# Attention with taps of a depthwise convolution in its gaps: another account of free VectorE time, taps a step behind a chunk's first operation, the check's sums of reciprocals later

## The chip, the core and the metric

The kernel runs on one core of a Trainium2 chip. The metric is the time of one execution on the device, in microseconds (us), lower is better. The engines that matter here are TensorE (PE; its weight loads are PEld), VectorE (DVE) and ScalarE (ACT). They run side by side and wait for each other through semaphores; each takes its own instructions in the order in which the program issued them.

## What is computed

Four layers are applied one after the other to x, 16 frames of 384 channels of 16 × 16 pixels in fp32. The change concerns the first layer (attention) and the depthwise convolution of the second, which is worked on in the attention's gaps. The later layers are shortened here:

```python
# layer 0: attention over 2 groups of 8 frames, N = 8*16*16 = 2048 tokens, 12 heads of 32
qk = (xt @ qk_w.T).reshape(B, N, 2, nh, HEAD_DIM)        # q, k projected; v is x itself
attn = softmax(einsum('bhnd,bhmd->bhnm', q * scale, k))
out = einsum('bhnm,bhmd->bhnd', alpha * eye + beta * attn - gamma / N, v)
# layer 1: depthwise 7x7 convolution, layer norm over channels, MLP 384 -> 1536 -> 384
y = conv7x7_depthwise(x) + dw_b
y = layernorm(y) * ln_g + ln_b
y = gelu(y @ w1 + b1)
gx = sqrt(sum(y**2 over the frame)); y = grn_g * (y * gx / mean(gx)) + grn_b + y
x = x + y @ w2 + b2
# layer 2: Sobel filters in x and y, 768 -> 384 projection, layer norm, gelu, residual
# layer 3: 1x1, depthwise 3x3, 1x1; linear attention with 8 heads; MLP 384 -> 1536 -> 384
```

## The kernel before

The image is cut into two batches b of four blocks of 512 columns (two frames); a block has three chunks of 128 channels. The program writes out its instructions in a fixed order per engine (`InOrder`, L86), so the place where the Python code issues an instruction decides what stands behind what.

**The attention** (`attention`, L368) runs over six units u = 0 to 5. A unit is a batch and a group of four heads. Each unit has four blocks n of queries, and each block 16 steps t of 128 keys, so there are 384 steps. In a step, `scores` issues the score matmuls of four heads into two PSUM tiles `st` (three such tiles exist, of two banks each), and ScalarE takes the exponentials into two `e` tiles (eight exist, so four steps). `weighted`, issued one step later, multiplies the exponentials with the values into `av`, and VectorE adds the `e` tiles up in chunks of four steps (`ADDS`), two additions of 128 × 1024 in each step but the first of a chunk. The sums go through matmuls with ones (`weights`) into the denominators `dn`, in four parts, each issued some steps later through the table `due`, which maps a step number to functions.

At a block's end `finish` (L508) copies the denominators to `r`, and hands to `due` four inversions of 128 columns each on VectorE (indices 2 to 5 of the next block), `scale` at index 6 (va times r), and `put` at 7 (the output block). `scale` also issues the check's sum on ScalarE: an Identity over `r` into `junk` that adds up the reciprocals. These sums end in a flag that says whether a second, general version has to be run. In the steps of `SLOTS` a projection for q or k is made; it uses one of the three `st` tiles, which ScalarE (q) or VectorE (k) frees by a copy.

**The filler.** After each step `fill` (L1444) issues work of the next layer. `conv` is a task that yields operations in order: for a chunk, one operation on ScalarE (the middle tap with bias, into y) and then 48 taps on VectorE, each one `scalar_tensor_tensor` on y. In the attention it does the two first blocks, 288 taps. How many are issued at a step is set by `room`, an account in microseconds: it gains 2.25 per step and what a projection adds, loses 2.28 for the two additions and 0.8 in steps 3 to 8 of a block for the inversions, and is cut at 3.0; every operation costs 0.57. `lead` is the first block's layer 1 after its convolution (sum over channels by a matmul `su`, centring y<-su, squares, second matmul `sv`, root with two table loads, inversion of 128 × 512, product, affine); one of its operations is issued at every fourth step. `su` and `sv` take one of the `st` tiles until they are read.

**After the attention** `plan.all` (L1508) orders everything else. `Plan` (L117) keeps when each engine will be free by set costs, and the tasks are taken by start time; among those that start within `SLACK` of the earliest, the lowest `RANK` goes first. There are tasks `l1`, `mid` and `l3c` per block (layer 1, layer 2 with the first parts of layer 3, the last MLP), `conv` for the taps that are left, `prepare` for weights, and `safety` for the flag. The eight turns of the two MLPs over the blocks are fixed (`TURNS`).

Of the kernel before, what the change touches and what calls it, by code (L numbers as in the profile page):

```python
# [11 lines left out]
ALU = mybir.AluOpType  # L12
# [5 lines left out]
NC = C // P  # L18
# [10 lines left out]
NBLK = N // BLK  # L29
NIP = NBLK  # L30
NQC = N // P
SLOTS = ((0, 4, 8), (0, 4), (0, 4), (0,))
FIRST = NQC + 10
# [11 lines left out]
AFTER = ('hid', 0, 2, 1)  # L45

RANK = {
    "mid": ((-4.2, 20.2, -65.9, 40.3), (11.6, 63.7, 50.6, 36.1)),
    "l1": ((-28.5, 90.6, 6.7, 64.2), (55.1, 56.5, 16.9, 27.6)),
    "l3c": ((32.8, 24.4, 106.0, 83.3), (3.4, 80.2, 74.5, 60.5)),  # L50
    "conv": 93.3,
}
SLACK = 0.142
JUNK = 2
ADDS = ((4, 4, 4, 4), (4, 4, 4, 4))
XB, YB, SB = 12, 2, 22
TB = BLK // P
RB = 2 * HW
# [132 lines left out]
            self.step(min((s for s in starts if s[0] <= first), key=lambda s: (s[1], s[0]))[2])  # L191


class Task:


    def __init__(self, name, rank, ops):
        self.name, self.rank, self.ops = name, rank, ops
        self.head = next(ops, None)

    def advance(self):
        self.head = next(self.ops, None)


def channel_means(dve, pool, X, cols, b):
# [162 lines left out]
def attention(tc, X, xt, L0, block, small, col, cols, ones, load_qk, banks, fill, bound):  # L368
# [4 lines left out]
    pe, act, dve = (InOrder(tc, e) for e in (nc.tensor, nc.scalar, nc.vector))  # L373
    units = [(b, g) for b in range(NB) for g in range(NC)]
    with ExitStack() as actx:
# [5 lines left out]
        op = pool("op", 2)  # L381
# [44 lines left out]
        due = {}  # L426

        def unit(u, made, gm):

            b, g = units[u]  # L430
            q, keys, v = made["q"], made["k"], made["v"]
            adds = ADDS[b]
            acc, sums = {}, {}

            def scores(n, t):
                es = []
                for i in range(2):
                    es.append(ep.tile([P, 2, BLK], F32, tag="e", name=f"e_{u}_{n}_{t}_{i}"))
                sts = [bank2(f"st_{u}_{n}_{t}_{i}") for i in range(2)]
                for h in range(4):  # L440
                    rows = slice(HD * h, HD * (h + 1))
                    pe.matmul(
                        sts[h // 2][:, h % 2, :],
                        keys[t // TB][rows, ts(t % TB, P)],
                        q[n][rows, :],
                        start=True,
                        stop=True,
                    )
                for i in range(2):
                    act.activation(es[i], sts[i], AF.Exp, scale=HD**-0.5)  # L450
                return es

            def weighted(n, t, es):
                if t == 0:
                    acc["av"] = pacc.tile([P, BLK], F32, tag="av", name=f"av_{u}_{n}")
                for h in range(4):
                    pe.matmul(
                        acc["av"][HD * h : HD * (h + 1), :],
                        v[t // TB][:, (t % TB) * P + HD * h : (t % TB) * P + HD * (h + 1)],
                        es[h // 2][:, h % 2, :],  # L460
                        start=(t == 0),
                        stop=(t == NQC - 1),
                    )
                at = t % adds[n]
                for i in range(2):
                    if at == 0:
                        sums[i] = es[i]
                    elif at == 1:
                        s = sp.tile([P, 2, BLK], F32, tag="s", name=f"s_{u}_{n}_{t}_{i}")
                        dve.tensor_tensor(s, sums[i], es[i], ALU.add)  # L470
                        sums[i] = s
                    else:
                        dve.tensor_tensor(sums[i], sums[i], es[i], ALU.add)


                k = (u * NBLK + n) * NQC + t
                if at == adds[n] - 1:
                    parts = 1 if t == NQC - 1 else adds[n]
                    for i in range(parts):
                        due.setdefault(k + 2 + i, []).append(  # L480
                            lambda i=i, summed=dict(sums): weights(
                                n, t, summed, ts(i, BLK // parts)
                            )
                        )
                for f in due.pop(k, ()):
                    f()
                if t == NQC - 1:
                    va = op.tile([P, BLK], F32, tag="va", name=f"va_{u}_{n}")
                    act.activation(va, acc["av"], AF.Copy, scale=1.0)
                    xg = op.tile([P, BLK], F32, tag="xg", name=f"xg_{u}_{n}")  # L490
                    act.activation(
                        xg, X[b][n][:, g, :], AF.Identity, scale=col("alpha", g), bias=gm
                    )
                    due[k + 2].append(lambda: finish(n, va, xg))

            def weights(n, t, summed, at):
                if t == adds[n] - 1 and at.start == 0:
                    acc["dn"] = pacc.tile([P, BLK], F32, tag="dn", name=f"dn_{u}_{n}")
                for h in range(4):
                    pe.matmul(  # L500
                        acc["dn"][HD * h : HD * (h + 1), at],
                        ones[:, :HD],
                        summed[h // 2][:, h % 2, at],
                        start=(t == adds[n] - 1 and at.start == 0),
                        stop=(t == NQC - 1),
                    )

            def finish(n, va, xg):  # L508

                if g == 0:  # L510
                    L0[b][n] = block(f"l0_{b}_{n}")
                k = u * NBLK + n
                r = op.tile([P, BLK], F32, tag="r", name=f"r_{u}_{n}")
                act.activation(r, acc["dn"], AF.Identity, accum_out=bound[:, 0, k : k + 1])

                def invert(i):
                    dve.reciprocal(r[:, ts(i, P)], r[:, ts(i, P)])

                def scale():
                    junk = op.tile([P, BLK], F32, tag="junk", name=f"junk_{u}_{n}", bufs=1)  # L520
                    act.activation(junk, r, AF.Identity, accum_out=bound[:, 1, k : k + 1])
                    dve.tensor_tensor(va, va, r, ALU.mult)

                def put():
                    dve.scalar_tensor_tensor(
                        L0[b][n][:, g, :], va, col("beta", g), xg, ALU.mult, ALU.add
                    )

                todo = [*(lambda i=i: invert(i) for i in range(TB)), scale, put]
                for i, f in enumerate(todo):  # L530
                    due.setdefault((k + 1) * NQC + 2 + i, []).append(f)

            return scores, weighted
# [9 lines left out]
        for u, (b, g) in enumerate(units):  # L543
# [5 lines left out]
            for n in range(NBLK):  # L549
                for t in range(NQC):  # L550
                    es = scores(n, t)
                    added = 0.0
# [3 lines left out]
                    if t in SLOTS[n]:  # L556
                        added = steps.pop(0)() if steps else 0.0
# [10 lines left out]
def conv_seq_kernel(  # L568
# [100 lines left out]
    pe, act, dve = (InOrder(tc, e) for e in (nc.tensor, nc.scalar, nc.vector))  # L669
# [30 lines left out]
    plan = Plan({"s": SB, "mm": 8, "x": XB - 2 * NBLK, "y": YB, "wa": NC, "wb": NC})  # L700
# [720 lines left out]
    conv = Task("conv", RANK["conv"], convolutions())  # L1421
# [14 lines left out]
    lead = next(t for t in tasks if t.name == "l1_0_0")  # L1436

    if fast:
        open_pool("s", SB)
        open_pool("tiny", 2)  # L1440

        room = 0.0

        def fill(t, added=0.0):  # L1444
            nonlocal room
            if t < 0:
                while plan.step(bias):
                    pass
                return


            if t % NQC == 9 and t > NQC:
                u, i = divmod(t // NQC - 1, NBLK)
                plan.mark(("l0", u // NC, i, u % NC))
            room = min(3.0, room + 2.25 + added - 2.28 * (t % 4 != 1) - 0.8 * (2 < t % NQC < 9))
            if NC * NBLK * NQC - 36 < t <= NC * NBLK * NQC - 21 and t % 3 == 0:
                room -= 1.7
            if ("y", 0, 0, NC - 1) in plan.made and t % 4 == 1 and plan.holds(lead, "wa"):
                room -= lead.head.length if lead.head.engine == "DVE" else 0.0
                plan.step(lead)  # L1460
            while t >= FIRST and room > 0 and ("y", 0, YB - 1, NC - 1) not in plan.made:
                if not plan.step(conv):
                    break
                room -= 0.57

        attention(
            tc, X, xt, L0, block, small, col, cols, ones, first_loads, banks, fill, bound
        )
    else:
        attention_general(tc, X, L0, block, col, cols, ident, first_loads)  # L1470
        open_pool("s", SB)
        open_pool("tiny", 2)
# [33 lines left out]
    if fast:  # L1506
        tasks.append(Task("safety", 99, safety()))
    plan.all(tasks, SLACK)  # L1508

# [90 lines left out]
```

## Time and profile before

| | us |
|---|---|
| median of three runs | 2695.55 (2694.98 to 2695.66) |
| the profiled execution | 2696.76 |
| its span, first to last instruction | 2695.0 |
| attention, first to last score matmul | 22.6 to 1056.1 |

Groups of the profile that the change touches, within the attention (count and mean of one):

| engine | group | count | ns each |
|---|---|---|---|
| VectorE | s<-s,e and s<-e,e, additions | 574 | 1209, 1216 |
| VectorE | r<-r, inversion of 128 columns | 92 | 938 |
| VectorE | y<-l,vec,y, taps | 279 | 472 to 721 |
| VectorE | va<-va,r and l<-va,vec,xg | 23 each | 682, 743 |
| VectorE | k<-pk, key copy | 21 | 674 |
| ScalarE | e<-st, exponentials | 767 | 1022 |
| ScalarE | junk<-r, the check's sum, and its accumulator read | 23 each | 633, 197 |
| ScalarE | y<-l,vec, first operation of a chunk | 6 | 814 |

In a line of the timeline, the first two numbers are start and duration; in brackets stands how long the engine was idle before and what it waited for. In the windows, each engine has its busy time and its number of instructions. PEclk is the granted TensorE clock as a share of full speed. All instructions issued through the ordered helpers carry line 96, so they are told apart by tile names: `st` scores, `e` exponentials, `av` weighted values, `dn` denominators, `pk` and `pq` projections, `y` the convolution, `ph` and `po` the two matmul groups of an MLP.

### The profile page before, as it was taken

What the parts mean: (1) busy time and instruction counts of PE and PEld (TensorE: products, weight loads), DVE (VectorE), ACT (ScalarE), POOL (GpSimd) and SP (SyncE); (2) the same over time, 40 slices, a digit from 0 to 9 for tenths busy, and PEclk for the clock granted to TensorE, in tenths of its full rate; (3) what the DMA queues carried; (4) which work ended last, traced back from release to release, by engine and by line L of the source; (5) the groups of instructions that cost most, each with busy time, mean ns of one, the idle gap of its engine ahead of it and who ended that gap; (6) DMA issues with size and microseconds to landing.
All of it is one profiled execution on the core that took longest, in us unless ns stands there. A gap on an engine that the chain in (4) does not pass through costs nothing. (4 is left out here: it accounts for less than half of the span.)

```text
span 2695.0 us, 33760 instructions
## 1 busy us (share of the span) xinstructions
PE 2656.3 (99%) x13477; PEld 1069.1 (40%) x13477; DVE 1996.9 (74%) x2586; ACT 1560.4 (58%) x2282; POOL 7.4 (0%) x54
## 2 busy tenths in 40 slices
PE   9999999999999999999999999999999999999999
PEld 3333333333332323445444444444454444454443
DVE  5899999999999989799999669999904535313120
ACT  5787787778877787565645372533665633125221
POOL 0000000000000000000000000000000000000000
PEclk9999999999999999999999999999999999999999
DMA  3000000000000002100111112121000110000000
GB/s 149 1 17 1 5 13 1 13 5 2 16 1 1 13 1 95 35 0 1 36 36 36 39 46 68 59 71 47 16 8 0 35 36 0 12 1 13 12 4 21
DMA packets 34421, 65.17 MB, mean 24 GB/s; under 512 B 1872, under 2 KB 17360, under 8 KB 34256
## 3 DMA queue, kind: packets, MB, share of 16 engines
q1 hardware_dynamic: 34112, 62.79, 7.1%
q8 instruction: 107, 1.75, 0.3%
q14 instruction: 58, 0.48, 0.1%
q10 hardware_dynamic: 144, 0.15, 0.0%
HBM read 56.64 MB, written 6.29 MB: 23 GB/s over the span
## 5 line engine op out<-in xcount | busy, mean ns | idle before, releaser
L96 ACT ACTIVATE e<-st 128x1024 f32<-128x1024 f32 x768 | 743.5, 1022 | 175.5 <-PE st L96 169.7
L96 DVE SCALAR_TENSOR_TENSOR y<-l,vec,y 128x420 f32<-128x420 f32 (+8 forms) x1152 | 658.9, 632 | 18.8 <-ACT y L96 13.4
L96 PE MATMUL st<-q,k 32*128 32x512 f32 x3072 | 464.5, 643 | 8.6 <-DVE k L96 3.3
L96 DVE TENSOR_TENSOR s<-s,e 128x1024 f32<-128x1024 f32 x384 | 444.8, 1209 | 2.8 <-ACT e L96 2.8
L96 PE MATMUL av<-e,v 128*32 128x512 f32 x3072 | 411.9, 607 | 0.7 <-ACT va L96 0.7
L96 PE MATMUL po_l<-hid_l,wb 128*128 128x512 f32 x576 | 258.2, 602 | 7.3 <-ACT hid_l L96 7.2
L96 PE MATMUL ph_l<-y,wa 128*128 128x512 f32 x576 | 258.6, 594 | 1.0 <-ACT y L96 1.0
L96 PE MATMUL ph_l3c<-d_l3c,wa 128*128 128x512 f32 x576 | 257.2, 593 | 0.0
L96 PE MATMUL po_l3c<-hid_l3c,wb 128*128 128x512 f32 x576 | 254.1, 593 | 0.0
L96 DVE TENSOR_TENSOR s<-e,e 128x1024 f32<-128x1024 f32 x192 | 225.6, 1216 | 33.0 <-PE dn L96 19.3
L96 ACT ACTIVATE hid_l3c<-ph_l3c,vec 128x512 f32<-128x512 f32 x96 | 65.8, 686 | 248.0 <-PE ph_l3c L96 247.8
L96 PEld LDWEIGHTS st<-q,k 32*128 32x128 f32 x3072 | 137.1, 183 | 170.3 <-issue 99.9
L96 PEld LDWEIGHTS av<-e,v 128*32 128x32 f32 x3072 | 60.6, 108 | 294.0 <-issue 286.1
L96 PEld LDWEIGHTS po_l<-hid_l,wb 128*128 128x128 f32 x576 | 110.4, 193 | 145.9 <-issue 131.5
L96 PEld LDWEIGHTS ph_l3c<-d_l3c,wa 128*128 128x128 f32 x576 | 108.9, 190 | 136.5 <-issue 129.8
L96 PEld LDWEIGHTS ph_l<-y,wa 128*128 128x128 f32 x576 | 108.3, 190 | 137.2 <-issue 126.2
L96 PEld LDWEIGHTS po_l3c<-hid_l3c,wb 128*128 128x128 f32 x576 | 108.7, 190 | 133.2 <-issue 129.6
L96 PEld LDWEIGHTS dn<-s,ones 128*32 128x32 f32 x2496 | 81.8, 111 | 187.4 <-issue 174.5
L96 DVE SCALAR_TENSOR_TENSOR o_l3c<-po_l3c,vec,l 128x512 f32<-128x512 f32 x24 | 17.6, 742 | 170.7 <-PE po_l3c L96 170.0
L96 PE MATMUL dn<-s,ones 128*32 128x128 f32 (+1 forms) x2496 | 142.4, 299 | 0.0
L96 ACT ACT_TABLE_LOAD x103 | 132.1, 1283 | 7.5 <-PE ph_l L96 5.4
L96 ACT ACTIVATE hid_l<-ph_l,vec 128x512 f32<-128x512 f32 x96 | 65.6, 683 | 119.4 <-PE ph_l L96 118.8
(155 smaller groups left out, 2480.5 us busy)
## 6 DMA issues: line engine op xcount, KB each, us to landing
wa<-in_w_dram SPq DMA_DIRECT2D x12, 768.0 KB, 4.5
wb<-in_w_dram SPq DMA_DIRECT2D x12, 768.0 KB, 4.6
wa<-in_mlp_w_dram SPq DMA_DIRECT2D x12, 768.0 KB, 4.5
wb<-in_mlp_w_dram SPq DMA_DIRECT2D x12, 768.0 KB, 4.5
x<-in_x_dram SPq DMA_DIRECT2D x8, 768.0 KB, 10.7
v<-in_xt_dram SPq DMA_DIRECT2D x24, 256.0 KB, 2.7
out_dram<-o_l3c SPq DMA_DIRECT2D x24, 256.0 KB, 2.0
qkv<-in_qkv_wT_dram SPq DMA_DIRECT2D x3, 576.0 KB, 11.1
```

The costliest lines, as they stand in the source:

```text
L96: self.last = self.tc.keep_in_program_order(make(*args, **kw))
```

## The change

Five things change. The account in `fill` is new: `pace` gives, for each step, the length of the step on TensorE and the work that VectorE has in it; `free` is their difference less the `lag` that VectorE carries over, and taps are issued only while at least 0.4 us is free, each at its own planned length, and 0.12 more if it depends on the tap before it in the same step. What is overdrawn becomes the next step's lag. When a chunk's first operation on ScalarE is issued, the loop ends, so its taps begin a step later. Lead operations are charged only when they were issued. The channel reductions, which lie three steps apart, are charged in the steps with remainder 1 instead of 0. The check's `junk` sum goes to its own function at index 8 of the list, that is index 10 of the block. `ADDS` is written per block of a batch's unit instead of per batch, with the same value 4 everywhere, so that the parts of the denominators come at the same steps. Three ranks, the rank of `conv` and `SLACK` have other numbers.

```diff
 RANK = {
-    "mid": ((-4.2, 20.2, -65.9, 40.3), (11.6, 63.7, 50.6, 36.1)),
-    "l1": ((-28.5, 90.6, 6.7, 64.2), (55.1, 56.5, 16.9, 27.6)),
+    "mid": ((-2.0, 20.2, -65.9, 40.3), (11.6, 63.7, 50.6, 36.1)),
+    "l1": ((-41.0, 15.6, 6.7, 64.2), (55.1, 56.5, 16.9, 27.6)),
     "l3c": ((32.8, 24.4, 106.0, 83.3), (3.4, 80.2, 74.5, 60.5)),
-    "conv": 93.3,
+    "conv": 100.5,
 }
-SLACK = 0.142
+SLACK = 0.151
-ADDS = ((4, 4, 4, 4), (4, 4, 4, 4))
+ADDS = (4,) * 24
...
+def pace(t):
+    n, i = divmod(t - 1, NQC)
+    adds = ADDS[n]
+    stride = adds // 4
+    pe, dve = 2.066, 2.275 if t and i % adds else 0.0
+    at = i - adds - 1
+    if at >= 0 and at % adds % stride == 0 and at % adds < 4 * stride and i > adds:
+        pe += 0.22
+    elif i == 1 and n > 0:
+        pe += 0.87
+    else:
+        pe += 0.09
+    if n > 0:
+        dve += {2: 0.88, 3: 0.88, 4: 0.88, 5: 0.88, 6: 0.6, 7: 0.66}.get(i, 0.0)
+    return pe, dve
...
 class Task:
...
     def advance(self):
-        self.head = next(self.ops, None)
+        self.at, self.head = self.head, next(self.ops, None)
...
-            adds = ADDS[b]
+            adds = ADDS[u * NBLK : (u + 1) * NBLK]
...
-                    parts = 1 if t == NQC - 1 else adds[n]
+                    parts = 1 if t == NQC - 1 else 4
                     for i in range(parts):
-                        due.setdefault(k + 2 + i, []).append(
+                        due.setdefault(k + 2 + i * adds[n] // 4, []).append(
...
                 def scale():
+                    dve.tensor_tensor(va, va, r, ALU.mult)
+
+                def check():
                     junk = op.tile([P, BLK], F32, tag="junk", name=f"junk_{u}_{n}", bufs=1)
                     act.activation(junk, r, AF.Identity, accum_out=bound[:, 1, k : k + 1])
-                    dve.tensor_tensor(va, va, r, ALU.mult)
...
-                for i, f in enumerate(todo):
+                for i, f in [*enumerate(todo), (8, check)]:
                     due.setdefault((k + 1) * NQC + 2 + i, []).append(f)
...
-            room = min(3.0, room + 2.25 + added - 2.28 * (t % 4 != 1) - 0.8 * (2 < t % NQC < 9))
-            if NC * NBLK * NQC - 36 < t <= NC * NBLK * NQC - 21 and t % 3 == 0:
-                room -= 1.7
+            length, work = pace(t)
+            free = length + added - work - lag
+            if NC * NBLK * NQC - 36 < t <= NC * NBLK * NQC - 21 and t % 3 == 1:
+                free -= 1.7
             if ("y", 0, 0, NC - 1) in plan.made and t % 4 == 1 and plan.holds(lead, "wa"):
-                room -= lead.head.length if lead.head.engine == "DVE" else 0.0
-                plan.step(lead)
-            while t >= FIRST and room > 0 and ("y", 0, YB - 1, NC - 1) not in plan.made:
+                if plan.step(lead) and lead.at.engine == "DVE":
+                    free -= lead.at.length
+            ops = []
+            while t >= FIRST and ("y", 0, YB - 1, NC - 1) not in plan.made:
+                op = conv.head
+                if op.engine == "DVE":
+                    if free < 0.4:
+                        break
+                    free -= op.length + 0.12 * (op.after[0] in ops[-1:])
                 if not plan.step(conv):
                     break
-                room -= 0.57
+                ops.append(op)
+                if op.engine == "ACT" and conv.head.engine == "DVE":
+                    break
+            lag = max(0.0, -free)
```

More of the change, by code (lines that the diff above doesn't have):

```diff
@@ L191, in all @@
             self.step(min((s for s in starts if s[0] <= first), key=lambda s: (s[1], s[0]))[2])
+def pace(t):
[13 more added lines that the diff above has]
+    return pe, dve
 class Task:
     def __init__(self, name, rank, ops):
-        self.name, self.rank, self.ops = name, rank, ops
+        self.name, self.rank, self.ops, self.at = name, rank, ops, None
         self.head = next(ops, None)
     def advance(self):
-        self.head = next(self.ops, None)
+        self.at, self.head = self.head, next(self.ops, None)
 def channel_means(dve, pool, X, cols, b):
@@ L1440, in conv_seq_kernel @@
         open_pool("tiny", 2)
-        room = 0.0
+        lag = 0.0
         def fill(t, added=0.0):
-            nonlocal room
+            nonlocal lag
             if t < 0:
```

## The prediction

> **What bounds the kernel now.** I read the page first, then the windows, then the waits of one engine after the other, then the timeline around the worst steps. Part 1 of the page settles which engine matters:
>
> ```profile
> span 2695.0 us, 33760 instructions
> PE 2656.3 (99%) x13477; PEld 1069.1 (40%) x13477; DVE 1996.9 (74%) x2586; ACT 1560.4 (58%) x2282; POOL 7.4 (0%) x54
> ```
>
> TensorE has work 99% of the span, and the change takes no matmul away. So it can only win back time in which TensorE stands still or runs slowly. The windows over the attention's first five units (64 steps each, the same work in each except that unit 0 begins with less) show where that is:
>
> ```profile
> core 0: us, PE busy (x) PEld busy (x) DVE busy (x) ACT busy (x) POOL busy (x), PEclk, DMA share, GB/s
> 22.60:194.16 171.56, 170.18 (x1457) 53.74 (x1456) 149.75 (x154) 133.18 (x151) 0.00 (x0) 1.00 0.05 16
> 194.16:367.09 172.93, 172.54 (x1492) 54.63 (x1488) 165.45 (x184) 136.35 (x158) 0.00 (x0) 1.00 0.03 7
> 367.09:542.74 175.65, 173.18 (x1492) 54.60 (x1488) 165.53 (x177) 136.27 (x158) 0.00 (x0) 0.99 0.03 7
> 542.74:714.17 171.43, 171.43 (x1493) 54.63 (x1489) 161.76 (x183) 137.20 (x159) 0.00 (x0) 1.00 0.03 7
> 714.17:892.51 178.34, 175.08 (x1494) 55.48 (x1491) 163.76 (x183) 137.04 (x159) 0.00 (x0) 0.99 0.01 3
> ```
>
> Unit 3 takes 171.4 us, units 1, 2 and 4 take 1.5, 4.2 and 6.9 us more for the same matmuls. Step by step (start of one group of score matmuls to the next) an undisturbed step takes 2.285 us, 5.06 with a projection in it. Over 383 steps the excess above each kind's shortest step is 37.2 us. 5.5 us of it is 0.23 us in step 6 of nearly every block, whatever stands around it, and stays. The waits name the causes of the rest:
>
> ```profile
> PE st L96 <- DVE k L96: 3.3, 3, 2.0
> PE st L96 <- DVE y L96: 3.3, 1, 3.3
> ACT junk L96 <- DVE r L96: 9.0, 8, 3.5
> DVE y L96 <- ACT y L96: 13.4, 7, 3.7
> ```
>
> The columns are microseconds in all, times, and the longest. Scores wait for VectorE's late key copy; the check's `junk` holds ScalarE until VectorE has inverted; VectorE itself waits at the first tap of each chunk for ScalarE. The timeline of unit 0, block 3 shows the second:
>
> ```profile
> 175.51 0.94 DVE L96 RECIPROCAL r<-r 128x128 f32<-128x128 f32 x1
> 176.49 0.63 ACT L96 ACTIVATE junk<-r 128x512 f32<-128x512 f32 x1 [1.27 <-DVE r L96]
> 177.11 3.75 ACT L96 ACTIVATE e<-st 128x1024 f32<-128x1024 f32 x4
> 178.17 0.30 PEld L96 LDWEIGHTS st<-q,k 32*128 32x128 f32 x4 [1.20 <-ACT e L96]
> ```
>
> The exponentials of the next step stand behind `junk`; TensorE's step 9 becomes 3.77 us long. The worst single step is the lead task's, where a PSUM bank stays taken until VectorE centres y:
>
> ```profile
> 873.07 1.75 DVE L96 SCALAR_TENSOR_TENSOR y<-su_l,y 128x1536 f32<-128x1536 f32 x1
> 874.87 0.30 PEld L96 LDWEIGHTS st<-q,k 32*128 32x128 f32 x4 [4.08 <-DVE y L96]
> ```
>
> **What the Trainium skill says.** "PSUM — Partial Sum Buffer", section Engine vs sequencer instructions: the queues of ScalarE and VectorE are strict FIFO. The lines above agree: four exponentials start at 177.11, when `junk` leaves. "TensorE: Matmul & The Clock Gate", Part 1: after an idle window of about 3.4 us (3413 ns, free running) the clock drops to half. Agreed: after the 3.26 us wait eight av matmuls that took 1.06 us take 1.94. A long stall costs up to 1.7 us on top. "ScalarE: Activation LUTs", What ACT_TABLE_LOAD costs, gives 1283 ns for a load; the trace has 1283.
>
> **Part 1: the check at due index 10 instead of 6.** It removes no instruction: 24 `junk` of 0.63 us and their accumulator reads of 0.20 move from due index 6 to 10. By then the last inversion, due at 5, lies five steps back. Steps 9 with a wait lost 0.73, 1.49, 0.47, 1.21, 0.80, 1.50, 0.18 and 0.76 us = 7.1 us. Steps 9 in which `junk` waited for nothing still lost 0.11, ScalarE's extra 0.83; I let that move to the later step. Gain 7.1 − 8 × 0.11 = 6.3 us; bounds 5.4 (ScalarE's own idle in the attention) and 7.1.
>
> **Part 2: the account with lag.** From the instruction lists of both kernels as built I sum VectorE's queue: what step s issues, minus the length of step s+1, carried on. Prices: two adds 2.32, an inversion 0.94, va×r 0.68, the put 0.74, the key copy 0.63, the channel reduction 1.75, a tap 0.63 on average. Unit 0, block 1's last step to block 2's step 4:
> before: 8 taps + adds = 7.51 behind an old 1.84, minus 5.06, leaves 4.30; then 2.02, 1.41, 2.61, 4.32 (3 more taps), 2.25.
> after: 6 taps, 6.23 behind 0.26, leaves 1.43; then 0, 0.02, 1.22, 2.20, 0.13.
> At step 5 the scores want the bank that the key copy frees. In the blocks n = 2 of units 0 to 4 the old queue at step 4 is 2.25, 1.83, 3.22, 1.64, 0.69, and the loss 1.08, 0.37, 2.03, 0, 0 us: the limit lies between 1.64 and 1.83. The new queue is 0.13, 0.24, 0.99, 0.49, 0.46: all below. With the half clock behind the 2.03 (0.41 + 0.95) that is 4.8 us, of which I take 4.6. The corrected charge for the channel reductions (remainder 1, not 0) is in these lists.
>
> **Part 3: a chunk's taps a step behind.** Six chunk starts in the attention make VectorE wait 12.9 us; TensorE lost about 1.7 us in the steps after them. ScalarE's 0.81 us stays; I take 1.2 us, bounds 0 and 1.7.
>
> **Part 4: the lead task.** Its su matmul moves from unit 4, block 3, step 5 to unit 5, block 0, step 1; its root from unit 5, block 1, step 5 to block 2, step 1. The su stretch lost 8.0 us (0.86 of it the matmul), because y<-su ran 3.3 us after its bank was wanted. In the new place the queue one step before is 0.7 us instead of 3.0, and a projection lengthens step 4, so the wait nearly goes; but su and the projection then hold two of three banks. I take 4.5 us, bounds 0 and 5.5. The root stretch lost 7.4 us. Root plus two loads (0.69 + 2 × 1.28 = 3.3 us on ScalarE) come directly behind va and xg (1.4), and the 3.34 us inversion lands where VectorE already has its four: my queue goes to 7.0 and 9.5 us at steps 6 and 7. The e tiles cover four steps, 9 us. I take +1.3 us, bounds −2 and +3.
>
> **Part 5: what is left for later.** 270 taps are placed up to the last adds instead of 280; 19 instead of 9 are left: 10 × 0.63 = 6.3 us. Cover: VectorE is busy for 45.5 of 63 us from 1057 to 1120. After it the new list reaches the first edge filter 1.3 us of work later, since other taps are put behind it. Without the cover the 6.3 us would come before the first middle block and TensorE, waiting there already (3.4 us at 1188.6 for pc_l3a), would lose them. TensorE's gaps after 1057 sum to 16.6 us; ranks and SLACK reorder work between 1060 and about 1650. New order helps at 1072 (2.2 us waiting for su, now issued later) and puts gx ahead of four taps; y_1 is ready later. I take 0, bounds −5 and +8.
>
> **Sum.** 6.3 + 4.6 + 1.2 + 4.5 + 1.3 + 0 = 17.9 us. The profiled execution took 2696.76, its span 2695.0; the median is 2695.55, so the execution is representative. 2695.6 − 17.9 = 2677.7, rounded to 2678. The bounds add to 1 and 25 if all fell on one side; half of either side gives 2670 to 2686.
>
> **Rivals.** (a) Only the check and the key copies gain; the lead costs what it did or more, and the later stage eats a little: 2695.6 − 10.9 + 3 = 2688. For it: both lead stretches depend on banks and ScalarE, which the account doesn't count. (b) The lead's stalls and their half clocks go too, and the later gaps shrink: 2678 − 12 = 2666. Against it: ScalarE still needs 3.3 us at one place. (c) Slower: the taps left over make VectorE late at the turns. It is 98% busy from 1120 to 1500 and from 1600 to 1900; if three turns each wait the 6.3 us and a half clock (1.7), TensorE loses 24 us: 2678 + 24 = 2702. It decides once the turns' loss passes 18 us. Against it: the new list is only 1.3 us behind at the edge filter, and VectorE is idle half the time from 1500 to 1600. (d) Not what it says: the stalls were ScalarE's and move on with `junk`: about 2695.
>
> **Chances.** Forecast 0.55, (a) 0.17, (b) 0.10, (c) 0.10, (d) 0.08. Beyond 0.2% (5.4 us, about what can be told from no change) faster: 0.55 + 0.10 + about 0.13 of (a) = 0.78; same: the rest of (a), most of (d) = 0.11; slower 0.11. The range takes in (b) and (a) and most of (d): 2665 to 2693.
>
> **What would show it.** `junk` waits for nothing; "PE st <- DVE k" gone; units 1 and 2 within 1 us of 171.5; the wait of VectorE for ScalarE's y below 3 us; unit 4 near 172, unit 5 carrying both lead stretches with 6 to 10 us. It is wrong if unit 5 grows by as much as unit 4 loses, or if TensorE's gaps after the attention exceed 16.6 us by more than 10.

## The result and the profile after

The changed kernel takes 2678.52 us (median of four executions, 2678.03 to 2679.67), the kernel before 2695.27 in the same comparison. The ratio is 0.9939, with a 95% interval of 0.9922 to 0.9956: 16.8 us less. The profiled execution took 2678.47 us.

The first part of its page (span; busy time and share of each engine):

```profile
span 2676.6 us, 33769 instructions
PE 2644.7 (99%) x13477; PEld 1066.7 (40%) x13477; DVE 1994.4 (75%) x2586; ACT 1559.3 (58%) x2281; POOL 7.4 (0%) x54
```

The matmuls are as many as before (13477). TensorE is busy 11.6 us less for the same work, for two reasons. A part of every stall is counted as busy (a score group that waits for a bank is shown with 2.0 us instead of 1.14), and matmuls at half clock take longer. The six units of the attention in the windows (borders at the first score matmul of each unit):

```profile
core 0: us, PE busy (x) PEld busy (x) DVE busy (x) ACT busy (x) POOL busy (x), PEclk, DMA share, GB/s
21.96:190.57 168.61, 168.61 (x1458) 53.61 (x1457) 145.79 (x149) 133.15 (x151) 0.00 (x0) 1.00 0.05 17
190.57:361.17 170.60, 170.60 (x1493) 54.18 (x1489) 162.56 (x179) 136.44 (x158) 0.00 (x0) 1.00 0.03 7
361.17:532.36 171.19, 170.77 (x1493) 54.37 (x1489) 163.94 (x175) 136.44 (x158) 0.00 (x0) 1.00 0.03 8
532.36:702.91 170.55, 170.33 (x1492) 54.05 (x1489) 161.63 (x182) 137.13 (x159) 0.00 (x0) 1.00 0.02 7
702.91:873.66 170.75, 170.75 (x1493) 54.41 (x1489) 163.56 (x186) 136.21 (x158) 0.00 (x0) 1.00 0.01 3
873.66:1038.90 165.24, 163.67 (x1442) 51.56 (x1439) 152.18 (x153) 138.83 (x163) 0.00 (x0) 1.00 0.02 6
```

Units 0 to 4 are now within 0.7 us of each other where they do the same work (unit 0 lacks the first chunk), and PEclk is 1.00 in all of them: no half clock is left in the attention. Before, the granted clock was half there three times for 3.41 us, at 480, 876 and 961 us. Where the same waits appear without it in another trace (the check alone, below), the steps are 1.6 us shorter at each of two such places; so the three together are an estimated 4.7 us of the gain. Unit 4, the worst before, needs 7.6 us less. Unit 5 took 163.07 us before and takes 165.24: it has both stretches of the lead task now. Measured step by step as in the prediction, the time above each kind's shortest step (a kind is a place in the block, with or without a projection) is by unit:

| unit | 0 | 1 | 2 | 3 | 4 | 5 | sum |
|---|---|---|---|---|---|---|---|
| before, us | 4.7 | 3.9 | 6.6 | 2.4 | 9.3 | 10.2 | 37.2 |
| after, us | 1.7 | 1.6 | 2.2 | 1.5 | 1.7 | 12.4 | 21.0 |

The spans differ by 18.4 us: 16.0 in the attention, 0.6 in its earlier start, and 1.7 in the stretch after it. (Before's profiled execution was 1.5 us above its median, which is most of the difference to the medians' 16.8.) Of the waits, those of ScalarE for VectorE and of TensorE for VectorE (total, times, longest):

```profile
ACT junk L97 <- DVE r L97: 3.5, 1, 3.5
```
```profile
PE st L97 <- DVE k L97: 0.6, 2, 0.4
PE st L97 <- DVE y L97: 0.6, 1, 0.6
```

The junk wait that is left, 3.5 us at 1049 us, belongs to the last block's check, behind the last scores; the 9.0 us before contained the same wait (3.5 at 1066 us). Inside the attention junk waits for nothing now. Before:

```profile
ACT junk L96 <- DVE r L96: 5.4, 7, 1.3
```

The key copy's wait fell from 3.3 to 0.6 us, the wait behind y<-su from 3.3 to 0.6. VectorE's wait for ScalarE's y, 12.9 us before, is gone. So the signs that the prediction named came true but for one: the wait for the key copy is smaller, not gone.

### The profile page after: what moved, and what is told of

The parts are those of the page before. It is cut to its first block, busy times and chain, and to the rows that moved or that the text cites. A ratio compares the mean times of both kernels' runs of the same rounds, so it can differ in the third digit from the quotient of the medians.

```text
span 2676.6 us, 33769 instructions
## 1 busy us (share of the span) xinstructions
PE 2644.7 (99%) x13477; PEld 1066.7 (40%) x13477; DVE 1994.4 (75%) x2586; ACT 1559.3 (58%) x2281; POOL 7.4 (0%) x54
## 5 line engine op out<-in xcount | busy, mean ns | idle before, releaser
L97 PE MATMUL st<-q,k 32*128 32x512 f32 x3072 | 457.8, 640 | 1.5 <-DVE k L97 0.6
L97 PEld LDWEIGHTS st<-q,k 32*128 32x128 f32 x3072 | 135.7, 183 | 159.7 <-issue 100.5
L97 ACT ACT_TABLE_LOAD x102 | 130.9, 1283 | 10.3 <-PE ph_l L97 7.4
## 6 DMA issues: line engine op xcount, KB each, us to landing
x<-in_x_dram SPq DMA_DIRECT2D x8, 768.0 KB, 10.8
```

Of the source, the lines that this page charges most:

```text
L97: self.last = self.tc.keep_in_program_order(make(*args, **kw))
```

## The experiments

Each ran beside the kernel before, in 5 to 21 executions. To read them together, each trace is split at the last score matmul: "attention" is from the first score group to the last, "later" from there to the end.

| kernel | median us | attention | later | taps left for later | conv's rank |
|---|---|---|---|---|---|
| before | 2695.3 to 2695.6 | 1033.0 | 1639.4 | 9 | 93.3 |
| after | 2678.5 | 1016.9 | 1637.7 | 19 | 100.5 |
| check alone moved | 2692.1 | 1027.8 | 1638.7 | 9 | 93.3 |
| after, check back | 2681.9 | 1019.6 | 1638.7 | 19 | 100.5 |
| account alone | 2685.5 | 1021.5 | 1640.4 | 16 | 93.3 |
| after, taps from free 0.0 | 2709.1 | 1019.6 | 1663.4 | 0 | 100.5 |
| after, no stop | 2692.7 | 1018.7 | 1650.7 | 16 | 100.5 |
| the same, conv's rank of before | 2680.9 | 1017.2 | 1640.3 | 16 | 93.3 |
| after, ranks of before | 2689.7 | 1017.0 | 1647.4 | 19 | 93.3 |
| the same, but conv's rank of after | 2679.2 | 1017.0 | 1637.5 | 19 | 100.5 |
| after, no taps from step 330 | 2715.5 | 1016.9 | 1674.2 | 33 | 100.5 |
| after, reader one step later | 2677.3 | 1015.2 | 1638.6 | 19 | 100.5 |
| after, root without tables | 2676.3 | 1014.9 | 1637.3 | 19 | 100.5 |
| after, reader in the same step | 2675.4 | 1012.6 | 1638.1 | 19 | 100.5 |

### The check

First alone, in the kernel before:

```diff
-                    act.activation(junk, r, ...)        # in scale(), due index 6
+                def check(): act.activation(junk, r, ...)
...
+                for i, f in [*enumerate(todo), (8, check)]:
```

> The kernel before with only the check's sums moved from due index 6 to 10. My theory (the exponentials of step 9 stood behind junk, and nothing takes its place): the eight waits with 7.1 us go and at most eight times 0.11 us move on, so 2695.3 - 6.3 = 2689.0, or 2687.4 if the 0.11 us go too as the trace of the changed kernel suggests; step 9 of the blocks at its shortest length. Rival (ScalarE is short of time at that place, the wait moves on with junk): step 13 or 14 grows by what step 9 loses, 2695. The key copies (3.3 us) and the lead's stretches (8.0 and 7.4 us) stay as they were under both.

Measured: 2692.09 us (2690.71 to 2693.44), ratio 0.9988 (0.9981 to 0.9995): 3.4 us. Step 9 did lose its excess, all 7.9 us outside the lead's stretch, and junk waits for nothing in the attention. But 22 steps 13, three after the new place, now lose 0.11 us each = 2.4 (before, none did); three steps 10 lose 0.68, 0.40 and 0.70 us; and one step waits 0.7 us longer for a key copy. (The trace's attention is 5.2 us shorter, more than the medians say. That is the half clock: at su it lasts 6.83 us in this trace, not 3.41, which costs 1.5; at the two other places it is missing, after the same waits of TensorE of 1.96 and 0.94 us, which saves 3.2.) The timeline of unit 0, block 3, one step after the place that the prediction showed (PEld's line, then PE's):

```profile
181.30 0.14 PEld L96 LDWEIGHTS dn<-s,ones 128*32 128x32 f32 x4 [0.54 <-DVE s L96]
```
```profile
181.31 0.41 PE L96 MATMUL dn<-s,ones 128*32 128x128 f32 x4 [0.27 <-DVE s L96]
```

The denominators' matmuls wait for the sums of VectorE. The three steps 10 are in the three blocks where junk had waited longest (1.27, 0.99 and 1.28 us). So VectorE itself was late there, and the stall behind junk had given it time to catch up. Take the stall away, and the next consumer of VectorE waits. Then the reverse, in the changed kernel:

```diff
                 def scale():
+                    act.activation(junk, r, ...)
                     dve.tensor_tensor(va, va, r, ALU.mult)
```

> The changed kernel with only the check's sums back at due index 6. If the parts add up as my prediction had it: 2678.5 + 6.3 = 2684.8. Theory now (the waits of junk are VectorE's late inversions, so the account alone had already cut them: with the account and the old place, the step 9 lost 3.1 us in units 0 to 3 and 2.1 beside the lead, where before it lost 7.1): 2678.5 + 3 to 5 = 2681.5 to 2683.5, with junk waiting for r by that much. Rival (the place of the check is worth what moving it alone gave, 3.4): 2681.9; the trace tells the two apart by which blocks' junk waits.

Measured: 2681.93 us (2680.74 to 2683.10), 3.4 us above the changed kernel. Step 9 loses 0.92, 0.92, 0.38, 0.71 and 0.65 us in units 0 to 4 = 3.6, and 1.5 in unit 5. So with the account in place, half of the junk waits are already gone. The check's new place takes the other half, and 1.2 us in eleven more steps 9 with 0.11 each, and pays 2.2 us in the steps 13. Its worth is 3.4 us in either company, within a spread of 1.2 to 1.4 us on either side.

### The account

The account with its lag, but the check in its old place, the old ranks, and no stop after a chunk's first operation:

```diff
-            room = min(3.0, room + 2.25 + added - 2.28 * (t % 4 != 1) - 0.8 * (2 < t % NQC < 9))
+            length, work = pace(t)
+            free = length + added - work - lag
...
+            lag = max(0.0, -free)
```

> The changed kernel's account (pace, lag, the lead charged when issued) with the old place of the check, the old ranks and SLACK, and without the stop after a chunk's first operation. My theory: key copies 4.6 (4.1 by the trace of the changed kernel) + su stretch 4.5 + root stretch 1.3 = 10.4 us, so 2684.9, with the check's 7 us still in step 9. Rival A (the parts lean on each other: with junk in its old place ScalarE has no room in unit 5): 5 us or less, 2690. Rival B (the stop, not the account, keeps the queue short): key copies as before, 2690 with the lead's gain alone.

Measured: 2685.53 us (2682.12 to 2686.38), ratio 0.9959 (0.9946 to 0.9973): 9.9 us. TensorE's wait for k falls to 0.4 us, the lead's two stretches from 15.4 to 9.0 (2.4 and 6.6, a half clock of about 1.6 in the latter), and what junk costs in the steps 9 of units 0 to 3 with a wait from 7.1 to 3.1. VectorE's wait at a chunk's first tap, 12.9 us before, is down to 2.7, without the stop. The prediction had counted on the stop to remove that wait. Which part of the account does it was not taken apart.

Then one number of the account, so that all 288 taps fit into the attention:

```diff
-                    if free < 0.4:
+                    if free < 0.0:
```

> The changed kernel with one number changed: a tap is issued while free is at least 0.0 instead of 0.4. All 288 taps then lie in the attention (19 more), and my sum of VectorE's queue grows to 2.4, 3.6 and 6.9 us at step 4 of block 2 of units 2, 3 and 4. My theory (the key copy wants its queue below about 1.7 us, and a wait once paid shortens the queue for good): TensorE loses about what stands above 1.7 us at the end of unit 4, 7.7 - 1.7 = 6 us, and a half clock or two (1.7 each): 2685 to 2688, with the line of scores waiting for VectorE's k back at about 6 us. Rival (the queue is not what delays the copy, and taps left over cost something later): 2678.5 - up to 8 = 2671 to 2678.

Measured: 2709.12 us (2707.52 to 2711.92), ratio 1.0056 (1.0042 to 1.0070): 30.6 us above the changed kernel. The wait for k is back at 3.7 us, and the attention is only 2.6 us longer, less than expected. By the traces another 25.7 us are lost later, and with nothing left to do. VectorE's timeline after the attention:

```profile
1076.89 1.75 DVE L97 TENSOR_TENSOR y<-y,s_l 128x1536 f32<-128x1536 f32 x1
1114.92 0.18 DVE L97 TENSOR_REDUCE gs_l<-gx_l 128x2 f32<-128x24 f32 x1 [36.27 <-ACT gx_l L97]
1115.62 1.27 DVE L97 SCALAR_TENSOR_TENSOR y<-l,vec,y 128x338 f32<-128x338 f32 x2 [0.53 <-ACT y L97]
...
1198.47 16.80 DVE L97 SCALAR_TENSOR_TENSOR y<-l,vec,y 128x392 f32<-128x392 f32 x31
1215.21 14.80 DVE L97 SCALAR_TENSOR_TENSOR g_l3a<-h_l3a,dw,g_l3a 128x450 f32<-128x450 f32 x24
```
```profile
1228.91 6.43 PE L97 MATMUL pd_l3a<-g_l3a,cb 128*128 128x512 f32 x8 [11.44 <-issue]
```

VectorE stands still for 36.3 us. There are two y tiles (`YB`), both full, and the third block's taps begin as soon as the first block's gx is read (1114.92). In the changed kernel that read comes at 1086.66: there the second block is not ready so early, so TensorE does the first block's first matmul group without the second's in between. Later that time is missing: 31 taps stand before g_l3a, and TensorE waits 11.4 us at pd_l3a (the profile names no releaser; pd starts when g_l3a is almost through). A second loss is a pair of waits at pg and po near 1341 us (5.33 and 3.89), which the ranks, below, explain. In all TensorE's gaps after the attention add up to 38.6 us, not 16.6, and the granted clock is half for 39.7 us there, not 15.8: the eight pd matmuls behind the long wait take 6.43 us. Twelve microseconds of taps moved into the attention won nothing afterwards and lost 25.7.

### The stop after a chunk's first operation

```diff
-                if op.engine == "ACT" and conv.head.engine == "DVE":
-                    break
```

> The changed kernel without the stop after a chunk's first operation, so that the first tap is issued in the same step. My prediction's part 3: 1.2 us, 2679.7, VectorE's waits for ScalarE's y back at about 13 us; bounds 0 and 1.7. Rival (the stop also keeps the queue short and moves the lead by four steps or more, as the queue sums show for unit 4): 3 us or more, 2681.5 and up, with what differs lying in unit 4's last block and unit 5.

Measured: 2692.71 us (2691.69 to 2694.69), 14.2 us above the changed kernel. The prediction's 1.2 us is far off; the rival's "3 us or more" takes it in, but most of it lies elsewhere than the rival said. In the attention units 0 to 3 lose 1.70, 1.57, 2.15 and 1.55 us without the stop, 1.70, 1.56, 2.15 and 1.52 with it. VectorE's wait for y is 2.4 us (none with the stop). So in those units the stop does nothing that can be seen. Three taps more fit in, the lead starts earlier (its su stretch is back in unit 4's last block), and the later stretch grows by 13.0 us. The attention is 1.8 us longer in this trace; 1.6 of that is a half clock of 3.41 us at 965 us, which the next kernel's trace, with the same order of work in the attention, does not have. To see whether that comes from the planner's order, one rank was set back:

```diff
-                if op.engine == "ACT" and conv.head.engine == "DVE":
-                    break
...
-    "conv": 100.5,
+    "conv": 93.3,
```

> The changed kernel without the stop after a chunk's first operation (which alone gave 2692.7), and with the one rank of conv back from 100.5 to 93.3. Safety, the flag's few operations, has rank 99: this one number decides whether the flag goes ahead of the taps. Theory 1 (the stop is worth its 1.8 us of the attention, and the other 12 us are the planner's order, which needs the flag last when 272 taps are placed): 22.3 + 1018.7 + 1640.4 = 2681.4 span, 2682 median; the 5.3 us wait of pg near 1326 gone. Theory 2 (the stop itself, or the lead's earlier place, costs the later stretch): 2690 or more.

Measured: 2680.87 us (2680.58 to 2681.07): 11.8 us less by one number. What remains to the changed kernel is 2.4 us, 0.2 of it in the attention and 2.6 later by the traces.

### The ranks

```diff
-    "mid": ((-2.0, ...  "l1": ((-41.0, 15.6, ...  "conv": 100.5   SLACK = 0.151
+    "mid": ((-4.2, ...  "l1": ((-28.5, 90.6, ...  "conv": 93.3    SLACK = 0.142
```

> The changed kernel with the ranks and SLACK of before; nothing in the attention differs. My prediction's part 5: 0, so 2678.5. By the trace of the account alone, which had these ranks, the stretch after the attention is 2.7 us longer: 2681. Rival (the order after the attention hangs on how many taps are left, and the ranks were what kept the 19 taps from costing): plus 6 us or more, 2685 and up, with new gaps of TensorE before 1250 us.

Measured: 2689.71 us (2687.30 to 2691.82), 11.2 us above the changed kernel, with an attention that is the same to 0.1 us. The rival holds as to the order; the gaps that it expected before 1250 us lie near 1320. TensorE's timeline at a block's gx near 1320 us, first in this kernel, then in the changed one:

```profile
1306.14 2.84 PE L97 MATMUL pc_l3a<-l,ca 128*128 128x512 f32 x6
1308.82 2.74 PE L97 MATMUL ph_l<-y,wa 128*128 128x512 f32 x6
1311.39 2.74 PE L97 MATMUL pc_l3a<-l,ca 128*128 128x512 f32 x6
1313.97 2.74 PE L97 MATMUL ph_l<-y,wa 128*128 128x512 f32 x6
1316.55 2.74 PE L97 MATMUL pc_l3a<-l,ca 128*128 128x512 f32 x6
1319.12 1.02 PE L97 MATMUL su_l3c<-s_l3c,ones 128*128 128x512 f32 x2
1325.48 0.58 PE L97 MATMUL pg_l<-gs_l,ones 128*128 128x2 f32 x2 [5.34 <-DVE gs_l L97]
1329.96 15.40 PE L97 MATMUL po_l<-hid_l,wb 128*128 128x512 f32 x30 [3.90 <-ACT hid_l L97]
```
```profile
1309.77 2.74 PE L97 MATMUL ph_l<-y,wa 128*128 128x512 f32 x6
1312.34 2.74 PE L97 MATMUL pc_l3a<-l,ca 128*128 128x512 f32 x6
1314.92 1.02 PE L97 MATMUL su_l3c<-s_l3c,ones 128*128 128x512 f32 x2
1315.78 2.74 PE L97 MATMUL pc_l3a<-l,ca 128*128 128x512 f32 x6
1318.35 0.28 PE L97 MATMUL pg_l<-gs_l,ones 128*128 128x2 f32 x2
1318.49 2.82 PE L97 MATMUL pc_l3a<-l,ca 128*128 128x512 f32 x6
1321.15 24.20 PE L97 MATMUL po_l<-hid_l,wb 128*128 128x512 f32 x56
```

After the last ph, the root of gx, its sum and the inversion have to pass through ScalarE and VectorE before po can start. In the changed kernel three pc groups (2.74 us each) lie behind the last ph and cover that chain. With the old ranks two of them were spent between the ph groups and only one lies behind the last, and TensorE stands still for 5.34 + 3.90 = 9.2 us. The granted clock is half for 10.2 us from 1324 us on, and po's matmuls take 0.51 us each on average there, 0.43 in the changed kernel. The same pair of waits is at 1326 in the kernel without the stop (5.35 and 3.89). Which of the five numbers does it? Safety, the flag's few small operations, has rank 99, between conv's 93.3 and 100.5:

```diff
     "mid": ((-4.2, ...  "l1": ((-28.5, 90.6, ...  SLACK = 0.142
-    "conv": 93.3,
+    "conv": 100.5,
```

> The changed kernel with the ranks of mid and l1 and SLACK of before, but conv's rank left at 100.5, above safety's 99. Theory 1 (of the five numbers only conv's place against safety matters): 2678.5, the flag's operations near 1170 us. Theory 2 (the other four share in the 11.2 us that all five gave): between 2681 and 2690, with pg's wait of 5.3 us near 1320.

Measured: 2679.20 us (2678.01 to 2680.39): the changed kernel's time to 0.7 us, with the same gaps. The other four numbers do nothing that can be told from the spread. The last of the flag's operations in VectorE's timeline, with the ranks of before and in the changed kernel:

```profile
1548.58 0.13 DVE L97 CAST unsafe<-flag 1x1 int32<-1x1 f32 x1
```
```profile
1170.71 0.14 DVE L97 CAST unsafe<-flag 1x1 int32<-1x1 f32 x1
```

Four operations of 0.76 us in all go 330 to 380 us earlier, ahead of taps. They cost next to nothing themselves; but near 1310 us the pc groups stand elsewhere. That the planner's start times, moved by these operations, lead there is the likely way; the planner's own list was not followed step by step.

### Fewer taps in the attention

```diff
-            while t >= FIRST and ("y", 0, YB - 1, NC - 1) not in plan.made:
+            while FIRST <= t < 330 and ("y", 0, YB - 1, NC - 1) not in plan.made:
```

> The changed kernel with no tap issued from step 330 on, so 14 more are left for after the attention (33, not 19), 8.8 us of VectorE. Theory 1 (VectorE's idle time after the attention covers what is left): the later stretch is the same, the root stretch loses VectorE's queue; 2677 to 2679. Theory 2 (the cover ends at 19): 2678.5 + 8.8 = 2687, with su of the second block later by that. Theory 3 (the order that the planner finds changes with the number left, as with no taps left, where the stretch after the attention was 25.7 us longer): off by more than 10 us to one side, with other tile names in the gaps.

Measured: 2715.51 us (2715.21 to 2721.29), 37.0 us above the changed kernel. The third theory holds: TensorE's gaps after the attention add up to 42.5 us, not 16.6, and are spread over the whole stretch (5.0 us at po near 1314, 4.2 at zb near 1542, 7.2 at sv near 2058); the granted clock is half for 44.7 us there, not 15.8. The attention is the same to 0.01 us, root stretch included, though VectorE has no taps from step 330 on. So the five taps that stood in the root stretch are no part of it. The lead's inversion and the block's own were still in VectorE's queue, so this kernel does not rule out the queue as a whole.

### The lead task

What is left in unit 5 comes from su's and sv's bank and from ScalarE's root. First the reader of each matmul was issued one step behind it, not four:

```diff
-            if ("y", 0, 0, NC - 1) in plan.made and t % 4 == 1 and plan.holds(lead, "wa"):
+            follows = lead.at is not None and lead.at.engine == "PE"
+            if ("y", 0, 0, NC - 1) in plan.made and (t % 4 == 1 or follows) and plan.holds(lead, "wa"):
```

> The changed kernel with the operation after su and sv (the centring of y, the root) issued one step after the matmul instead of four, so that the bank is freed about 7 to 9 us earlier; the root comes at step 14, before the block's end, not behind va and xg. Theory 1 (the held bank makes the two stretches): the su stretch falls from 3.65 to about 1.2 us, the root stretch from 5.2 to about 2 us: 2678.5 - 5.5 = 2673. Theory 2 (the root's 3.3 us of ScalarE with its two table loads, and VectorE's queue of 9.5 us, make the second stretch): only su gains, 2 us, the root stretch stays at 4 to 5 us wherever it lies: 2676.5. If the early root meets a fuller VectorE or ScalarE: no gain, 2678 to 2681.

Measured: 2677.32 us (2676.05 to 2677.79); attention 1.7 us shorter. The su stretch is 2.5 us (it was 3.65), the root stretch 4.1 (5.2). That is nearer to theory 2, the more so as 5.2 is counted too high: steps 1 and 2 of a block without a projection take 2.58 and 3.31 us when nothing disturbs them (unit 5, block 3), 0.7 more than the shortest of their place, and that 0.7 is in the changed kernel's root stretch (and in the 7.4 before), but not in this one's. (The table by unit has it three times in unit 5, before and after alike.) So the root stretch gained 0.4 us, not 1.1.

Then the root's two parts apart, with a plain copy in the root's place, which leaves out the square root of the first block and with it the two table loads:

```diff
-        act.activation(s[1], sv, AF.Sqrt, scale=1.0 / C, bias=eps)
+        act.activation(s[1], sv, AF.Identity if name == "l1_0_0" else AF.Sqrt, scale=1.0 / C, bias=eps)
```

> The changed kernel with the lead's root replaced by a plain copy with scale and bias (so the first block's normalisation is not computed as in the reference): the operation stays at its step, its two table loads of 1.28 us go. Theory 1 (ScalarE's 3.3 us, most of it tables, delay the exponentials): the root stretch of 5.2 us falls to 2.6, which are sv's 1.1 and two steps with a bank less: 2676. Theory 2 (the bank held from step 13 to step 2 makes the stretch): it stays within 0.5 us of 5.2, 2678.5.

Measured: 2676.28 us (2675.61 to 2677.27), attention 2.0 us shorter. The root stretch is 3.6 us, between the two theories: two table loads of together 2.56 us on ScalarE cost TensorE 1.6 there (and 0.5 at step 10 of the same block, where the denominators had waited for VectorE's sums). Without the 0.7 the rest is 2.9: sv's own 1.1, and 1.8 of steps with a bank less. "ScalarE: Activation LUTs", What ACT_TABLE_LOAD costs, gives 1283 ns for one, and adds a drain of about 1380 ns for a switch of tables. The trace has 1.28 us for the load, and no such drain: in the timeline below the root starts 0.02 us after its load. A load's price on ScalarE is thus about 1.3 us here, and on TensorE's path 1.0. Last, the reader right behind its matmul:

```diff
-                if plan.step(lead) and lead.at.engine == "DVE":
+                stepped = plan.step(lead)
+                if stepped and lead.at.engine == "PE":
+                    plan.step(lead)
+                if stepped and lead.at.engine == "DVE":
```

> The changed kernel with the reader of su and of sv issued right behind the matmul, in the same step (one step later gave 2677.3 with 2.6 and 4.1 us in the two stretches). Theory 1 (what is left of the bank's hold still costs): su stretch 1.8, root stretch 3.2 us: 2675.8. Theory 2 (now ScalarE and VectorE wait at the head of their queues for su and sv, and the exponentials behind the root come later still): 2677.5 or more, with ScalarE's s_l waiting for sv.

Measured: 2675.36 us (2674.12 to 2676.83), ratio 0.9926 (0.9912 to 0.9939), the best of all: 3.2 us under the changed kernel, whose executions (2678.03 and up) do not overlap with these, though the two were not run in one comparison. Attention 4.3 us shorter. Its timeline at su and at the root:

```profile
880.71 1.12 PE L97 MATMUL su_l<-s_l,ones 128*128 128x512 f32 x2
881.76 0.31 PEld L97 LDWEIGHTS st<-q,k 32*128 32x128 f32 x8 [0.76 <-ACT e L97]
881.87 1.76 DVE L97 SCALAR_TENSOR_TENSOR y<-su_l,y 128x1536 f32<-128x1536 f32 x1 [2.10 <-PE su_l L97]
...
944.65 1.28 ACT L97 ACT_TABLE_LOAD   x1
945.95 0.69 ACT L97 ACTIVATE s_l<-sv_l,eps 128x512 f32<-128x512 f32 x1
946.65 1.28 ACT L97 ACT_TABLE_LOAD   x1
947.95 3.77 ACT L97 ACTIVATE e<-st 128x1024 f32<-128x1024 f32 x4
949.03 1.13 PE L97 MATMUL st<-q,k 32*128 32x512 f32 x4 [0.81 <-ACT e L97]
```

y<-su starts 0.04 us after su ends; in the changed kernel it started at 892.92, 10.8 us after su's end. The su stretch is now su's own 1.06 us. The root stretch is 3.0: sv's 1.06 and once 1.92, where the exponentials come late behind the two loads. Not all of the 4.3 us is the bank: the reader's place moves the rest of the lead too, and step 10 of block 2 no longer loses its 0.6.

## Why the prediction was right, and where it was not

The forecast was 2678 with a range of 2665 to 2693; measured 2678.5. The sum of 17.9 us stands against 18.4 between the two profiled executions. That they agree so well is partly luck: the check was taken 2.9 us too high, the root and the stretch after the attention gave 0.9 and 1.7 us more than taken. Some terms were right for another reason, and one was right by an accident that the working did not see. Two sums of the working do not come out: with the key copies at 4.6, the bounds of its parts add up to 0 and 27 us, not 1 and 25, and half of the upper side gives 2673, not 2670. And of the 9.0 us that it read for junk, 3.5 lie behind the attention; its 7.1 us at step 9 do not contain them.

**The check (6.3 us).** Mis-sized: 3.4. The 7.1 us at step 9 were there, and they went. Two terms were mis-sized. Half of the 7.1 belongs to the account, which makes the inversions come in time (3.6 us were left for the move); and without the account the move gives part of it back at the next waits for VectorE (1.8 us in three steps 10). And the 0.11 us of ScalarE's extra time was counted for 8 blocks; at the new place it is lost in 22, also in blocks n = 0, where the projection of step 8 had covered it at the old one: 2.4 us instead of 0.9.

**The key copies (4.6).** In steps 3 to 7 of blocks n = 2, units 0 to 4 lost 5.5 us before and 1.5 after: 4.0 gained, 1.6 of it by the half clock behind the longest wait. The limit of 1.64 to 1.83 us for the queue did not hold: two copies with queues of 0.99 and 0.49 by the lists still cost 0.49 and 0.29 us. The lists take TensorE's steps at their shortest, so they may have put the old queue too high, where TensorE's own stalls gave VectorE time; that was not measured by itself. Checks and key copies together, 10.9 predicted, with the 1.2 below 12.1: units 0 to 4 without the su stretch lost 18.9 us before and 8.6 after, so 10.3.

**A chunk's taps a step behind (1.2).** Wrong cause: VectorE's wait for ScalarE's y is at 2.4 to 2.7 us without the stop as well, so the account removed most of it, and the stop only the last 2.4. In units 0 to 3 the stop is worth nothing; what remained of it once conv's rank was set back, 2.4 us, lies mainly in the order after the attention.

**The lead.** su: 4.5 predicted, 8.0 to 3.65 = 4.35 measured. Root: 1.3 predicted, 7.4 to 5.2 = 2.2 measured. Both lie in unit 5 with 8.9 us, within the 6 to 10 named. A part of both gains is the half clock that stood in each stretch before (about 1.5 us each, by the trace of the check alone) and is gone. VectorE's queue of 9.5 us cost little: in that block TensorE waits for VectorE's sums once, 0.6 us at step 10, and with the check in its old place junk waits there (1.5 us at step 9).

**What is left for later (0, bounds −5 and +8).** Measured −1.7 in the later stretch, with TensorE's gaps at 16.6 us as before; the granted clock was half for 15.8 us there, before for 22.3. The zero was nearly right, its reason was not. It counted taps as work that VectorE's idle time covers. The runs show that the number of taps left acts through the planner's order: with conv's rank at 100.5 the later stretch is 1663 us with 0 left, 1651 with 16, 1638 with 19, 1674 with 33; at 93.3 it is 1639 with 9, 1640 with 16, 1647 with 19. The changed rank and the changed account belong together, and the bounds, of +8 at most, were less than a quarter of the 36.5 us that the stretch cost more with 33. A half clock was priced at 1.7 us per stall there; behind the long gaps it lasted up to 10.2 us with 33 left and 13.7 with none. Rival (c) had the place right (the turns), and its 24 us are near the 25.7 of the kernel with no taps left, but by chance, since it took the work left over for the cause. In the kernel with the old ranks, what decides is which matmuls are left to cover a chain; for the kernel with 33 left each gap's own cause was not followed. The instruction order alone, without any time, would have shown that the flag's operations move from behind the first turns to ahead of them.

Whether other ranks would make 0 or 33 taps left as good as 19 was not tried, nor was the best kernel with ranks of its own.

## What to carry to other kernels

A stall can pay for another engine's lag: before counting it as a gain, ask whether the engine behind it is on time for its next consumer. In a program ordered by a planner, a change of what is left to it must be judged together with its priorities: an experiment that changes one of the two and keeps the other measures mostly the mismatch. A shared PSUM tile should be read right behind the matmul that fills it; here that was worth 3.2 us for two tiles, 2.6 of it at the first, where the stretch fell to the matmul's own 1.06.

## What the runs showed of the hardware

With sv holding one of the three st tiles, every second step took 0.87 us longer, at the same size each time, while the steps between were hardly longer (3.15, 2.29, 3.15, 2.35 with the account alone; 2.29 undisturbed). And an operation that waits at the head of VectorE's queue for a matmul (2.10 us idle before y<-su in the best kernel) cost nothing in the steps after it. The half clock came in stretches of 3.41 us and its multiples (up to 13.65 in the kernel with no taps left). In the attention of the kernel before it came after waits of TensorE that the trace shows as 1.96, 3.26 and 0.94 us. The same waits of 1.96 and 0.94 us were followed by none in the trace of the check alone, so one trace does not say what such a wait costs: with the half clock it is about 1.6 us more. All three waits are shorter than the idle window of 3.4 us that the prediction cites and calls agreed; as a part of each stall is counted as busy, the traces do not settle how long TensorE really stood.
